# Four chained image layers on one core: scans with their own buffers beside the layers of the next pair of images

## The chip, the cores and the metric

The kernel runs on one core of a Trainium2 chip. The metric is the device time of one execution in microseconds (us); the median of three runs of the kernel before is 18586.44 us (18541.16 to 18590.59). The engines are named as in the profile: PE (matrix products, with PEld for the loading of weights), DVE (vector), ACT (activation functions), POOL (GpSimd) and SP, which here only issues DMAs. Everything is in float32. Work arrays live in SBUF, results of PE land in PSUM (eight banks of 512 float32 for each of 128 partitions), and inputs, outputs and spilled arrays in the memory outside (DRAM).

## The reference

Eight images of 64 channels and 64 x 64 pixels go through four layers, one after the other:

```python
x = _L0_conv_ref(x, ...)   # softmax(x^T x / 8) over all 4096 pixels, weighted sum, 3x3 depthwise conv, 1x1 conv, + x
x = _L1_conv_ref(x, ...)   # two blocks of attention in windows of 8x8 (the second one shifted by 4), each with an MLP
x = _L2_conv_ref(x, ...)   # 9 taps weighted by a filter of the pixel and one of the channel, then a 1x9 convolution, + x
x = _L3_conv_ref(x, ...)   # norm, selective scan in four directions, gating, + x; then pooled depthwise convolutions
```

The scan of layer 3 works on 128 channels per image, four directions k (rows, columns, and both backwards) and 16 states per channel:

```python
h = h * jnp.exp(dt_t[..., None] * A) + dt_t[..., None] * B_t[:, :, None, :] * u_t[..., None]
return (h, jnp.einsum('bkcn,bkn->bkc', h, C_t))
```

over the 4096 pixels in the direction's order. dt is softplus of a projection of u; B and C are projections of u too.

## The kernel before

Two images at a time stand on the 128 partitions (64 channels each). `tile_kernel` (L1551) goes through the four pairs p, and for each runs `layer0_direct`, `layer1_direct`, `layer2` and `layer3` one after the other. Each layer opens its own pools of SBUF and PSUM, which take the place of the layer before; four large buffers ("slabs" of 66 x 66) are shared by all of them.

The kernel is written in a tile language: the source gives instructions with their tiles; a planner sets the order of each engine's queue from the data between instructions, the buffers that are free and its own estimate of durations, with the source's order as priority, and puts in the waits. On the chip each queue runs strictly in that order.

Layer 0 (L585) takes columns of the 4096 x 4096 scores in four blocks of 1024; for each of 32 row tiles PE makes the scores of both images (L637), ACT takes exp with a running sum (L647), and PE adds up the weighted values (L623). `block0` (L568) does the depthwise convolution with nine DVE instructions over the whole image (L433). Layer 1 (L733) goes through eight rows of windows in each of two blocks: `window_head` (L769) makes a norm, queries, keys and values, `window_row` (L819) scores, exp, weighted values and the projection; the head of the next row is called in the middle of the present row (L902). `mlp_direct` (L924) follows. Layer 2 (L1096) takes eight chunks of 512 pixels. Nearly all products of these layers are on PE; POOL has only borders and copies there.

Layer 3 norms (L1187), and then for each of the two images: `mixed` (L1201) makes the 128 channels XC of the scan, `ss2d_direct` (L1271) runs the scan, and `project_out` (L1245) makes the gate, the norm of the result Y and the projection. `safm` (L1488) ends the pair.

A scan has 32 units for an image: four directions of eight chunks of 512 pixels. `group_inputs` (L1302) makes, a unit ahead, dt and dt times u in `du` (L1310 to L1316; the product L1316 reads du and XC, both in SBUF), stores them to DRAM as `rows` (L1322, issued by ACT), and B and C by two further products (L1326, L1328). `group_scan` (L1332) then works in four quarters q. On the 128 partitions stand 16 states x 8 channels, so each channel's dt and dt u must be on 16 partitions: one DMA (L1356, issued by SP) reads 8 rows of 16 KB from `rows` with each row repeated for 16 partitions, 2 MB into `ub`, of which there are two buffers. POOL multiplies by B (L1364, 2048 elements a partition), ACT makes exp(dt A) into PSUM (L1369), DVE scans (L1371, four of 512), ACT keeps the last column as carry (L1373). The product with C is shared: POOL does half from SBUF (L1375), DVE the other half with a copy `pc` of C in PSUM (L1376, made by L1351). PE sums over states into `y` (L1378), and DVE adds y into Y (L1387, L1389), for directions along columns with a stride of 64.

Of the kernel before, what the change touches and what calls it, by code (L numbers as in the profile page):

```python
# [222 lines left out]
class _Net:  # L223
# [104 lines left out]
    def open(self, ctx, direct):  # L328

        pool = ctx.enter_context(self.tc.tile_pool(name="path", bufs=1))  # L330
        if direct:
            with self.tc.tile_pool(name="temp", bufs=1) as temp:
                self.load(temp, (3,))
                self.prepare_windows(pool)
        else:
            self.load(pool, (4,))
            self.prepare_general(pool)
        self.slabs = ctx.enter_context(self.tc.tile_pool(name="slabs", bufs=4 if direct else 5))
# [246 lines left out]
    def layer0_direct(self, p):  # L585

        nc, tc, w = self.nc, self.tc, self.w  # L590
        X = self.flat("X")
        nc.sync.dma_start(X, self.x[2 * p : 2 * p + 2].rearrange("b c h w -> (b c) (h w)"))
        pad = self.slab("att").rearrange("p (h w) -> p h w", w=66)
        self.pad_border(pad, 66)
        VT = self.flat("VT").rearrange("p (t c) -> p t c", c=P)
        NB = 1024
        with ExitStack() as st:
            wk = st.enter_context(tc.tile_pool(name="w0d", bufs=2))
            ps = st.enter_context(tc.tile_pool(name="ps0d", bufs=3, space=PSUM))
            pso = st.enter_context(tc.tile_pool(name="ps0o", bufs=1, space=PSUM))  # L600

            for g in range(4):
                pv = ps.tile([P, 8, P], F32, name="pvd", tag="s")
                for h in range(2):
                    nc.tensor.matmul(
                        pv[:, 4 * h : 4 * h + 4, :], lhsT=self.ones[0:1, :], rhs=self.b1row, start=True, stop=False
                    )
                    for j in range(4 * h, 4 * h + 4):
                        t = 8 * g + j
                        nc.tensor.matmul(  # L610
                            pv[:, j, :], lhsT=X[:, t * P : (t + 1) * P], rhs=self.w1bd, start=False, stop=(j % 4 == 3)
                        )
                nc.scalar.activation(VT[:, 8 * g : 8 * g + 8, :], pv, AF.Relu)

            parts = wk.tile([P, 2, 32, 4], F32, name="parts", tag="parts", bufs=1)
            half = (slice(0, 64), slice(64, 128))
            for jc in range(L // NB):
                po = pso.tile([P, NB], F32, name="pod", tag="po")

                def weigh(t, es):  # L620
                    for h in range(2):
                        for im in range(2):
                            nc.tensor.matmul(  # L623
                                po[half[im], h * CH : (h + 1) * CH],
                                lhsT=VT[:, t, half[im]],
                                rhs=es[im][:, h * CH : (h + 1) * CH],
                                start=(t == 0),
                                stop=(t == 31),
                            )

                last = None
                for t in range(32):
                    ss = [ps.tile([P, NB], F32, name=f"sd{im}", tag="s") for im in range(2)]
                    for h in range(2):
                        o = jc * NB + h * CH
                        for im in range(2):
                            nc.tensor.matmul(  # L637
                                ss[im][:, h * CH : (h + 1) * CH],
                                lhsT=X[half[im], t * P : (t + 1) * P],
                                rhs=X[half[im], o : o + CH],  # L640
                                start=True,
                                stop=True,
                            )
                    es = []
                    for im in range(2):
                        e = wk.tile([P, NB], F32, name="ed", tag="ed", bufs=6)
                        nc.scalar.activation(  # L647
                            e, ss[im], AF.Exp, scale=C**-0.5, accum_out=parts[:, im, t, jc : jc + 1]
                        )
                        es.append(e)  # L650
                    if last is not None:
                        weigh(*last)
                    last = (t, es)
                weigh(*last)
                nr = NB // 64
                nc.vector.tensor_copy(  # L656
                    pad[:, 1 + nr * jc : 1 + nr * (jc + 1), 1:65], po.rearrange("p (h w) -> p h w", w=64)
                )

            sums = self.sums[:, p]  # L660
            nc.vector.tensor_reduce(sums, parts, AX.X, ALU.add)
# [157 lines left out]
    def window_row(self, i, wy, T, now, ahead, wk, ps, pss, psa):  # L819
# [42 lines left out]
        def weigh(x, e):  # L862
# [14 lines left out]
            if x == x4 + 2:  # L877
                normalise(x4, av)
# [710 lines left out]
```

## Time and profile before

| what | value |
|---|---|
| median of 3 runs | 18586.44 us |
| the profiled execution: time, span | 18587.73 us, 18585.9 us |
| mean granted clock of PE | 0.690 |
| busy share of the span: PE, DVE, ACT, POOL | 60%, 47%, 34%, 38% |
| the two DMA queues of SP (q1) and ACT (q10), share of 16 engines' span | 52.8%, 2.2% |
| moved by DMA | 2311.16 MB |
| chain that ended last, by engine | PE 39%, DMA 21%, POOL 18%, DVE 14%, ACT 5%, issue 3% |
| POOL product with B, L1364: number, mean | 1024, 4614 ns |
| POOL product with C, L1375 | 1024, 2342 ns |
| DVE scans, L1371 | 3584 of 1264 ns and 512 of 1204 ns |
| DVE product with C, L1376 | 1024, 1219 ns |
| ACT exp of dt A, L1369 | 4096, 680 ns |

The table of groups in a profile gives for each line and engine how many instructions there were, the time in which at least one ran and the mean of one; PE overlaps its products, so its busy time is less than number times mean. The page cuts the span into 40 slices and gives the busy share of each in tenths; "granted clock" is the share of full speed that PE got. A second view gives the same for stretches that one chooses. The first pair of images takes the stretch from 26 to about 4630 us.

### The profile page before, as it was taken

The page shows a single profiled execution, that of the slowest core. Times are in us where ns is not written, and L with a number is a line of the kernel's source. Part 1 is how long each engine was busy: PE and PEld are TensorE (multiplying, and loading weights), DVE is VectorE, ACT ScalarE, POOL GpSimd, SP SyncE. Part 2 cuts the span into 40 slices and gives each one's busy share as a digit, 9 for nine tenths or more (in the row PEclk, how much of TensorE's full clock was granted, in tenths as well). Part 3 has the DMA queues.
Part 4 walks back from the last instruction along what each step waited for, and adds up shares of the span by engine and source line. Part 5 has one row for each costly group of instructions (what it writes and reads, how often), then busy time and mean ns, then how long its engine had stood idle before and what let it go on. Part 6 is the DMA issues. An engine that isn't in the chain of part 4 may idle for free.

```text
span 18585.9 us, 125685 instructions
## 1 busy us (share of the span) xinstructions
PE 11180.3 (60%) x47382; PEld 3532.5 (19%) x47382; DVE 8741.3 (47%) x8028; ACT 6383.0 (34%) x10722; POOL 7154.4 (38%) x2272
## 2 busy tenths in 40 slices
PE   9895444444989544444498954444459895444444
PEld 3441000001344100000134410000013441000001
DVE  0224665665032466566503246656650324665665
ACT  5432332332543233233255323323325432332332
POOL 0003664664000366466400036646630003664664
PEclk9777666666977666666697766666669766666666
DMA  0005996995000599699500059969950005996995
GB/s 15 1 1 114 213 208 153 214 209 128 1 1 1 115 211 208 153 213 208 129 1 1 1 120 213 209 151 212 209 124 1 1 1 114 213 208 151 212 209 128
DMA packets 221419, 2311.16 MB, mean 124 GB/s; under 512 B 19072, under 2 KB 19200, under 8 KB 88960
## 3 DMA queue, kind: packets, MB, share of 16 engines
q1 hardware_dynamic: 152640, 2164.33, 52.8%
q10 hardware_dynamic: 68160, 138.71, 2.2%
q8 instruction: 373, 6.11, 0.1%
q14 instruction: 246, 2.02, 0.0%
HBM read 2160.35 MB, written 142.61 MB: 124 GB/s over the span
## 4 chain that ended last, share of the span: by engine, by line
PE 39%; DMA 21%; POOL 18%; DVE 14%; ACT 5%; issue 3%; POOLq 0%; SPq 0%; ACTq 0%; DVEq 0%
DMA ub<-rows 21%; POOL vd L1364 13%; DVE hd L1371 9%; PE sd L637 5%; PE pod L623 5%; POOL vd L1375 5%; PE w_av L870 4%; PE pbd L1326 4%; PE yd L1378 3%; PE w_s L834 2%; PE pb L1165 2%; PE acc L1169 2%; PE py L1178 2%; DVE XC L433 2%; DVE cv L433 1%
## 5 line engine op out<-in xcount | busy, mean ns | idle before, releaser
L1378 PE MATMUL yd<-vd,pack 128*32 128x512 f32 x8192 | 3139.7, 1009 | 5708.5 <-POOL vd L1375 5708.1
L1371 DVE TENSOR_TENSOR_SCAN hd<-dad,carry,vd 128x512 f32<-128x512 f32 x3584 | 4306.7, 1264 | 2650.3 <-POOL vd L1364 2650.2
L1364 POOL TENSOR_TENSOR vd<-ub,BC 128x2048 f32<-128x2048 f32 x1024 | 4724.6, 4614 | 1384.4 <-DMA ub<-rows 1374.7
L1369 ACT ACTIVATE dad<-ub,As 128x512 f32<-128x512 f32 x4096 | 2663.9, 680 | 4535.9 <-DVE hd L1371 3676.8
L1375 POOL TENSOR_TENSOR vd<-hd,BC 128x1024 f32<-128x1024 f32 x1024 | 2398.0, 2342 | 3158.8 <-DVE hd L1371 3130.5
L1378 PEld LDWEIGHTS yd<-vd,pack 128*32 128x32 f32 x8192 | 375.1, 137 | 8366.1 <-POOL vd L1375 7291.6
L647 ACT ACTIVATE ed<-sd 128x1024 f32<-128x1024 f32 x1024 | 1039.2, 1020 | 871.3 <-PE sd L637 871.1
L1171 POOL MEMSET act<- 128x32 f32 x32 | 4.0, 125 | 3364.3 <-PE pf2d L938 2480.0
L1376 DVE TENSOR_TENSOR vd<-hd,pcd 128x1024 f32<-128x1024 f32 x1024 | 1248.4, 1219 | 70.3 <-DVE hd L1371 2.8
L637 PE MATMUL sd<-X 64*128 64x512 f32 x4096 | 1041.1, 619 | 7.5 <-ACT ed L647 7.5
L623 PE MATMUL pod<-ed,VT 128*64 128x512 f32 x4096 | 1000.3, 606 | 0.0
L1310 PE MATMUL pdd<-XC,xdt 128*128 128x512 f32 x512 | 470.9, 1013 | 824.7 <-ACT BC L1328 478.7
L417 POOL MEMSET XP<- 128x66 f32 x4 | 0.6, 154 | 2469.2 <-PE n_c L459 2469.2
L1326 PE MATMUL pbd<-XC,pack 128*128 128x512 f32 x1024 | 875.0, 986 | 18.6 <-ACT du L1315 18.6
L1373 ACT ACTIVATE carry<-hd 128x4 f32<-128x4 f32 x896 | 185.1, 207 | 1928.6 <-DVE hd L1371 1928.6
L1371 DVE TENSOR_TENSOR_SCAN hd<-dad,vd 128x512 f32<-128x512 f32 x512 | 584.4, 1204 | 553.0 <-POOL vd L1364 553.0
L870 PEld LDWEIGHTS w_av<-vals,w_e 64*64 64x64 f32 x16384 | 722.8, 174 | 286.3 <-issue 231.0
L656 DVE COPY att<-pod 128x1024 f32<-128x1024 f32 x16 | 19.6, 1226 | 1589.8 <-PE pod L623 1589.7
L870 PE MATMUL w_av<-vals,w_e 64*64 64x9 f32 x16384 | 749.6, 224 | 4.5 <-ACT w_e L859 3.6
L1328 ACT ACTIVATE BC<-pbd 128x512 f32<-128x512 f32 x512 | 305.2, 597 | 885.5 <-POOL vd L1364 646.4
L1389 DVE TENSOR_TENSOR Y<-Y,yd 128x512 f32<-128x512 f32 x192 | 207.2, 1079 | 718.4 <-PE yd L1378 718.3
L637 PEld LDWEIGHTS sd<-X 64*128 64x128 f32 x4096 | 362.2, 187 | 675.9 <-issue 655.1
(244 smaller groups left out, 11356.7 us busy)
## 6 DMA issues: line engine op xcount, KB each, us to landing
ub<-rows SPq DMA_DIRECT2D x1024, 2048.0 KB
rows<-du ACTq DMA_DIRECT2D x512, 256.0 KB
X<-in_x SPq DMA_DIRECT2D x4, 2048.0 KB
out<-Y SPq DMA_DIRECT2D x32, 256.0 KB
pack<-in_w ACTq DMA_DIRECT2D x1, 2691.0 KB
pack<-in_w ACTq DMA_DIRECT2D x1, 1193.0 KB
pack<-in_w ACTq DMA_DIRECT2D x1, 424.5 KB
pack<-in_w ACTq DMA_DIRECT2D x1, 66.0 KB
```

The source lines that it names most:

```text
L433: nc.vector.scalar_tensor_tensor(dst, src, wt[:, t : t + 1], dst, ALU.mult, ALU.add)
L623: nc.tensor.matmul(po[half[im], h * CH : (h + 1) * CH], lhsT=VT[:, t, half[im]], rhs=es[im][:, h * CH : (h + 1) * CH], start=(t == 0), sto ...
L637: nc.tensor.matmul(ss[im][:, h * CH : (h + 1) * CH], lhsT=X[half[im], t * P : (t + 1) * P], rhs=X[half[im], o : o + CH], start=True, stop= ...
L647: nc.scalar.activation(e, ss[im], AF.Exp, scale=C**-0.5, accum_out=parts[:, im, t, jc : jc + 1])
L870: nc.tensor.matmul(av[half[im], x - x4 + j, h, :], lhsT=e[half[im], h // 4, j, h % 4, :], rhs=V[half[im], x + j, h, :], start=True, stop=True,
L1326: nc.tensor.matmul(pb, lhsT=w[name][:, k, :], rhs=xc, start=True, stop=True)
L1364: nc.gpsimd.tensor_tensor(v, ub[:, 1], BB.unsqueeze(1).to_broadcast([P, 4, TD]), ALU.mult)
L1369: nc.scalar.activation(da, ub[:, 0, r], AF.Exp, scale=self.As[:, k, g : g + 1])
L1371: nc.vector.tensor_tensor_scan(along(h[:, r]), along(da), along(v[:, r]), first, ALU.mult, ALU.add)
L1375: nc.gpsimd.tensor_tensor(v[:, 0:2], h[:, 0:2], CC.unsqueeze(1).to_broadcast([P, 2, TD]), ALU.mult)
L1376: nc.vector.tensor_tensor(v[:, 2:4], h[:, 2:4], pc.unsqueeze(1).to_broadcast([P, 2, TD]), ALU.mult)
L1378: nc.tensor.matmul(y[32 * r : 32 * r + 32], lhsT=w["ysel"][:, q, :], rhs=v[:, r], start=(q == 0), stop=(q == 3))
```

## The change

A new class `_Direct` takes the place of the four layers' direct versions; `tile_kernel` calls the front of the next pair (layers 0 to 2 and the inputs of the scan) after the scans of the present one, and the end of layer 3 (`back`) after that.

- **Buffers.** Scans have SBUF and four PSUM banks of their own that stay open for the whole run (Y, carries, pool `scan`, `ps_scan`); the layers have three slabs and four other banks (three of tag f, one accumulator). Layer 0 now takes blocks of 512 columns in place of 1024, the scores of layer 1 two separate banks, the MLP a chunk at a time with norm, Gelu and the reloading of the table (`log_exp`) in each chunk. The next head of layer 1 is called at the end of a row, its queries have one buffer. Convolutions go by 16 rows.
- **Memory between.** The front stores x2 (layer 2's result), and for each image xc (the scan's channels), xt (the same with rows and columns exchanged, turned by an ACT copy) and zs (the gate). A scan loads its 512 columns from xc or xt, contiguous in both cases, and stores ys; `back` loads ys, zs and x2. Each has two buffers in DRAM.
- **Spread.** A quarter is cut in two (rp); each half has two DMAs (s) that read 4 KB rows, 0.5 MB each, into a `ub` of half the size. `rows` are stored by SP in place of ACT.
- **Products.** POOL multiplies 1024 elements at a time, takes three quarters of the product with C, and DVE one quarter; that one reads h and C, both in SBUF. The copy `pc` in PSUM is gone.
- Borders, the copy into XP and the enlarging of the pooled arrays move from POOL to DVE and ACT. The order of directions is 1, 3, 0, 2.

The core of the diff (the removed functions are those printed above; what is left out of layers 0 to 2 computes as before):

```diff
+class _Direct:
...
+        self.dram = ctx.enter_context(tc.tile_pool(name="mem", bufs=2, space=bass.MemoryType.DRAM))
+        one = ctx.enter_context(tc.tile_pool(name="scan1", bufs=1))
+        self.Y = one.tile([P, L], F32, name="Y", tag="Y")
+        self.carries = one.tile([P, 4, 4], F32, name="carry", tag="carry")
+        self.sw = ctx.enter_context(tc.tile_pool(name="scan", bufs=2))
+        self.slabs = ctx.enter_context(tc.tile_pool(name="slabs", bufs=3))
+        self.ps = ctx.enter_context(tc.tile_pool(name="ps_scan", bufs=3, space=PSUM))
+        self.pf = ctx.enter_context(tc.tile_pool(name="ps_front", bufs=3, space=PSUM))
...
+    def mlp(self, i, X, wk):
...
+            for im in range(2):
+                ph = self.bank("ph")
+                nc.tensor.matmul(ph, lhsT=w[f"f1w{i}"][half[im], :], rhs=H[half[im]], start=True, stop=True)
+                h = wk.tile([P, CH], F32, name="hid", tag="hid", bufs=4)
+                g = nc.scalar.activation(h, ph, AF.Gelu, bias=net.bf1[:, i : i + 1])
+                hid.append(h)
+            net.log_exp(g)
...
+    def scan_sources(self, p, X2):
...
+                for s in range(4):
+                    cv = wk.tile([P, 16, 64], F32, name="xcv", tag="xcv")
+                    self.dwconv(cv, pad, 16 * s, 16, w["cw"], w["cb"])
+                    nc.scalar.activation(cv, cv, AF.Silu)
+                    last = nc.scalar.activation(XT[:, 16 * s : 16 * s + 16, :], cv, AF.Copy)
+                    nc.sync.dma_start(xc[:, 1024 * s : 1024 * s + 1024], cv.rearrange("p a b -> p (a b)"))
...
+                    z = wk.tile([P, CH], F32, name="z", tag="z")
+                    last = nc.scalar.activation(z, pz, AF.Silu, bias=w["in_b"][:, 1:2])
+                    nc.sync.dma_start(zs[:, c * CH : (c + 1) * CH], z)
+                net.log_exp(last)
+                self.kept[2 * p + im] = (xc, xt, zs)
...
+    def scans(self, image):
+        xc, xt, _ = self.kept[image]
+        self.out = self.memory("ys")
+        units = []
+        for k in (1, 3, 0, 2):
+            order = range(NTD) if k < 2 else range(NTD - 1, -1, -1)
+            units += [(k, c, at) for at, c in enumerate(order)]
...
+    def inputs(self, image, unit):
...
+        x = wk.tile([P, TD], F32, name="xs", tag="xs")
+        nc.sync.dma_start(x, self.kept[image][k % 2][:, c * TD : (c + 1) * TD])
+
+        pd = ps.tile([P, TD], F32, name="pdd", tag="da")
+        nc.tensor.matmul(pd, lhsT=net.xdt[:, k, :], rhs=x, start=True, stop=True)
+        du = wk.tile([P, 2, TD], F32, name="du", tag="du", bufs=1)
+        nc.scalar.activation(pd, pd, AF.Exp, bias=w["dtb"][:, k : k + 1], accum_out=net.esum[:, image, k, c : c + 1])
+        nc.scalar.activation(du[:, 0], pd, AF.Ln, bias=1.0)
+        nc.vector.tensor_tensor(du[:, 1], du[:, 0], x, ALU.mult)
+
+        rows = self.dram.tile([32, 2, 4, TD], F32, name="rows", tag="rows")
+        for s in range(2):
+            nc.sync.dma_start(rows[:, s].rearrange("m r t -> r m t"), du[:, s])
...
+    def scan(self, nth, unit, ready, ahead):
...
+        for q in range(4):
+            for rp in range(2):
+                ub = wk.tile([P, 2, 2, TD], F32, name="ub", tag="ub")
+                for s in range(2):
+                    nc.sync.dma_start(
+                        ub[:, s].rearrange("p r t -> p (r t)"),
+                        rows[GD * q : GD * q + GD, s, 2 * rp : 2 * rp + 2]
+                        .rearrange("d r t -> d (r t)")
+                        .unsqueeze(0)
+                        .to_broadcast([NST, GD, 2 * TD]),
+                    )
+                v = wk.tile([P, 2, TD], F32, name="vd", tag="v", bufs=3)
+                nc.gpsimd.tensor_tensor(v, ub[:, 1], BB.unsqueeze(1).to_broadcast([P, 2, TD]), ALU.mult)
+                h = wk.tile([P, 2, TD], F32, name="hd", tag="h")
+                for j in range(2):
+                    r = 2 * rp + j
+                    da = ps.tile([P, TD], F32, name="dad", tag="da")
+                    nc.scalar.activation(da, ub[:, 0, j], AF.Exp, scale=net.As[:, k, 4 * r + q : 4 * r + q + 1])
+                    first = 0.0 if at == 0 else self.carries[:, q, r : r + 1]
+                    nc.vector.tensor_tensor_scan(along(h[:, j]), along(da), along(v[:, j]), first, ALU.mult, ALU.add)
...
+                if rp == 0:
+                    nc.gpsimd.tensor_tensor(v, h, CC.unsqueeze(1).to_broadcast([P, 2, TD]), ALU.mult)
+                else:
+                    nc.gpsimd.tensor_tensor(v[:, 0], h[:, 0], CC, ALU.mult)
+                    nc.vector.tensor_tensor(v[:, 1], h[:, 1], CC, ALU.mult)
...
+            if q == 1:
+                following = ahead()
...
+            o = wk.tile([P, TD], F32, name="yo", tag="yo", bufs=1)
+            nc.vector.tensor_tensor(self.img(o), yd, yp, ALU.add)
+            nc.sync.dma_start(self.out[:, c * TD : (c + 1) * TD], o)
...
+    def back(self, p):
...
+                nc.sync.dma_start(X[:, cols], self.kept["x", p][:, cols])
...
+                    nc.sync.dma_start(y, self.kept["y", 2 * p + im][:, cols])
+                    nc.sync.dma_start(z, self.kept[2 * p + im][2][:, cols])
...
 def tile_kernel(ctx: ExitStack, tc: tile.TileContext, x: bass.AP, packs, layout, out: bass.AP):
     net = _Net(ctx, tc, x, packs, layout, out)
     with ExitStack() as path:
         net.open(path, True)
+        d = _Direct(net, path)
+        net.log_exp()
+        d.front(0)
         for p in range(B // 2):
-            t = net.layer0_direct(p)
-            t = net.layer1_direct(t, p)
-            t = net.layer2(t)
-            net.layer3(t, p, True)
+            d.scans(2 * p)
+            d.scans(2 * p + 1)
+            if p + 1 < B // 2:
+                d.front(p + 1)
+            d.back(p)
```

Behind it, in both kernels, stands a second, general path that runs only where a sum of exponentials leaves its range; it doesn't run here.

## The prediction

> **What bounds the kernel now.** I read the 40 slices first, then cut the first pair of images into its stages with the table of busy times by stretch (front: layers 0 to 2 and the scan's inputs; scan of image 0; between; scan of image 1; end of layer 3).
>
> ```profile
> PE   9895444444989544444498954444459895444444
> ...
> DVE  0224665665032466566503246656650324665665
> ...
> POOL 0003664664000366466400036646630003664664
> ...
> DMA  0005996995000599699500059969950005996995
> ```
> ```profile
> 26.00:1601.00 1575.00, 1414.66 (x9037) 615.18 (x9037) 355.56 (x458) 618.24 (x971) 6.57 (x29) 0.82 0.01 2
> 1601.00:2973.00 1372.00, 599.74 (x1272) 103.47 (x1271) 830.27 (x700) 430.59 (x785) 885.18 (x255) 0.62 0.93 208
> 2973.00:3085.00 112.00, 58.51 (x89) 18.41 (x89) 66.82 (x46) 28.39 (x38) 2.86 (x5) 0.61 0.00 0
> 3085.00:4459.00 1374.00, 602.88 (x1280) 104.49 (x1280) 835.84 (x704) 432.88 (x786) 888.02 (x256) 0.63 0.92 208
> 4459.00:4630.00 171.00, 97.19 (x174) 34.11 (x175) 96.23 (x91) 48.53 (x74) 5.56 (x23) 0.72 0.07 25
> ```
>
> After the stretch and its length come busy us of PE, weight loads, DVE, ACT and POOL, then the granted clock, the DMA share and GB/s. The reader is to see two opposite halves. In the front PE is busy 1415 of 1575 us, while POOL and DMA stand still; in a scan the DMA engines are busy 93% of 1372 us, POOL and DVE some 60%, PE 44%. The pattern repeats four times. So today's bound alternates: PE and its chains for some 1,850 us of a pair's 4,604, the spread of dt (ub<-rows) for 2,746.
>
> The DMA rows price that spread:
>
> ```profile
> q1 hardware_dynamic: 152640, 2164.33, 52.8%
> q10 hardware_dynamic: 68160, 138.71, 2.2%
> ```
>
> q1 is SP's queue, nearly all of it ub: 0.528 x 18585.9 / 1024 = 9.58 us for one spread of 2 MB. q10 is ACT's: 0.022 x 18585.9 / 512 = 0.80 us for 256 KB in 2 KB rows. The load of X, also 2 MB in rows of 16 KB but each read once, keeps the queue busy 82.3% of 7 us (4508 to 4515), 5.8 us. So the spread is slow for its bytes, and it is the same row read by sixteen partitions.
>
> **What the change costs per unit.** A unit is one direction and chunk, 32 to an image, 64 to a pair; now 1372/32 = 42.9 us. I work out what each engine must do in a unit if the next pair's front is laid beside it.
>
> DMA now: 4 x 9.58 + 2 x 0.80 = 39.9 (93% of 42.9). Added: the load of xs, 256 KB, 0.80; and through memory x2 twice 2 MB for a pair, and for each image xc, xt, zs, ys written and ys, zs read, 12 MB, in all 28 MB: 112 x 0.80 = 90 us a pair, 1.4 a unit. The spread itself goes from rows of 16 KB to rows of 4 KB, a form the trace doesn't show. Its floor is X's rate, 5.8 us for 2 MB; its ceiling I set at today's 9.58, since the 2 KB rows of q10 (6.4 us for 2 MB) show no loss by short rows. I take 9.58: the same row is still read sixteen times. Sum 42.1; with the floor 27.0.
>
> POOL: 8 products of 1024 at half of L1364's 4.61 (2.31), 4 of 1024 at 2.34 and 4 of 512 at 1.17: 32.5, now 27.7.
>
> DVE: 830.3/32 = 25.9, less four L1376 of 1.22 plus four of 512 at 0.69 (L583's row), and du 1.36 to 0.69 now that x is contiguous: 23.1. The front and end add (355.6 + 66.8 + 96.2)/64 = 8.1: 31.2.
>
> ACT: 430.6/32 = 13.5, some four more carries at 0.21, less the two DMA issues that go to SP; front and end (618.2 + 28.4 + 48.5)/64 = 10.9. Layer 0's exps come in halves: 256 more a pair, with a readout of 0.20 each and two of about 0.60 (L1328's row for 512) for one of 1.02, 97 us a pair; two table loads of 1.28 in each of 16 MLP chunks, 41; the turned copies into XT, two of 4096 at L1217's 3.6, 7. Together 27.
>
> PE: 599.7/32 = 18.7, less pcd 396.8/256 = 1.55, plus (1414.7 + 58.5 + 97.2)/64 = 24.5: 41.7 at today's clocks.
>
> SP: 16 spreads, xs and two rows at 0.51 us to issue, 9.8 us, and some 105 issues of layers and back in a pair, 0.8: no bound. But all of them are now in one queue in order: a store of rows that waits for du, or of xc that waits for a convolution, has the next ub behind it, and POOL's product waits for that. The inputs of a unit are asked for two quarters ahead, some 20 us, which covers the new load of xs; uncovered, 256 x 3 us would be 770.
>
> **A wait that is added.** The second half of h x C moves from pcd, in PSUM, to CC, in SBUF, beside h in SBUF. The one DVE product in today's scan with both operands in SBUF is du:
>
> ```profile
> L1316 DVE TENSOR_TENSOR du<-du,XC x256: 685/1115/5073, 1604.2 to 18284.3; 128x512 f32<-128x512 f32 x128
> ...
> L1376 DVE TENSOR_TENSOR vd<-hd,pcd x1024: 1202/1222/1226, 1637.6 to 18404.9; 128x1024 f32<-128x1024 f32 x171
> ```
> ```profile
> 2005.88 4.53 POOL L1364 TENSOR_TENSOR vd<-ub,BC 128x2048 f32<-128x2048 f32 x1 [0.44 <-DMA ub<-rows]
> 2006.42 4.53 DVE L1316 TENSOR_TENSOR du<-du,XC 128x512 f32<-128x512 f32 x1
> ```
>
> The first fence gives least, median and greatest ns of two lines, the second start and us of two instructions. du takes 0.69 us at its shortest, 5.07 at its longest: begun 0.54 us into a product on POOL it ends 0.54 us after it. L1376, with PSUM, never stretches. So I charge each such operation half a POOL product, 1.17 us, and POOL the operation's own time. In a unit there are five (four CC, one du) and some 200 of the front's in a pair (convolution taps, sums), 3 a unit: DVE 31.2 + 8 x 1.17 = 40.6. POOL stands 5 x 0.69 plus 193/64 (four convolutions of 38 us and 40 us of sums) = 6.5: 39.0.
> The Trainium skill, SBUF — State Buffer, "Who interferes with whom", says the same against this change: a DVE instruction with two SBUF inputs and a GpSimd one that reads SBUF exclude each other for a whole instruction. Without that rule DVE would need 31 a unit and POOL 32.5, and the sum below would not move, since DMA decides it.
>
> PE's 41.7 holds at the clocks of the table above, 0.62 in a scan and 0.82 in the front. Over 60 to 550 us, where PE is busy 488 of 490, the granted clock is 1.00; at that clock in the mixed stage PE would need 17.2 x 0.62 + 24.5 x 0.82 = 31. I keep 31 and 41.7 as ends.
> TensorE: Matmul & The Clock Gate, Part 1, says that idleness throttles the array and activity releases it; by that rule PE, fed from two sides, would need 31 and drop out; the sum would again stay with DMA.
>
> **Does the order allow it?** The queues are in order, so the front can only fill gaps if the planner deals its instructions among the scan's. Today's trace shows that it does so where buffers allow:
>
> ```profile
> 4540.07 2.41 DVE L431 TENSOR_SCALAR S<-F,pack 128x4096 f32<-128x4096 f32 x1 [0.86 <-ACT F L1503]
> 4542.40 2.28 DVE L1514 TENSOR_TENSOR half<-F 128x2048 f32<-128x2048 f32 x1
> 4544.60 4.48 DVE L433 SCALAR_TENSOR_TENSOR S<-F,pack,S 128x4096 f32<-128x4096 f32 x1
> 4549.00 1.22 DVE L1518 TENSOR_TENSOR pool<-half 128x1024 f32<-128x1024 f32 x1
> ```
>
> In the source all nine taps of S stand ahead of half. The change gives scans and layers separate SBUF, four PSUM banks each and memory between, so nothing but data ties them; only z of the next pair (two buffers of zs) waits until back has read the present one.
>
> **Sum.** In the mixed stage DMA 42.1, PE up to 41.7, DVE 40.6 and POOL 39 lie together, so none runs at its bound. Today 39.9 gives 42.9, 8% over. With a spread buffer half as deep (2 x 1 MB) I take 46, a pair's 64 units 2,944 us. The first front stands alone: 1,575 plus 250 for three shared banks in place of eight, heads that follow the row (16 x 10 us) and the MLP's table loads, 1,825. The last pair's scans with back beside them: 64 x 44 = 2,816. Last back 171 + 20. Start 26. Sum 26 + 1,825 + 3 x 2,944 + 2,816 + 191 = 13,690. The profiled execution took 18587.73 (span 18585.9), the median of three is 18586.44; so 26% less.
>
> **Rivals.** (1) The spread in 4 KB rows is fast (X's rate): DMA 27; DVE and PE decide, 40 a unit mixed, POOL's 36 (32.5 + 3.5) plus one at the end: 26 + 1,825 + 7,680 + 2,368 + 191 = 12,090. For it: 9.58 against 5.8 for equal bytes. Against: the repetition stays. 0.25. (2) The front is a chain of short steps; each waits on an engine behind a scan or an exp, and it outlasts the scans: if every step waits as long as it works, 2 x 1,825 = 3,650 a pair, 26 + 1,825 + 10,950 + 2,816 + 191 = 15,810. For it: layer 1 is PE, DVE, ACT by turns with two or three banks. 0.22. (3) Slower, and the change not doing what it says: the planner places a pair's scans ahead of the whole next front on each queue. Then a pair is 1,825 + 2,816 + 191 = 4,832, four 19,350; it decides when less than 250 us of a front is hidden. Against it: the order above. 0.08. The forecast keeps 0.45.
>
> Range 11,700 to 16,000: both unknown spreads and the stretched front, without serial queues. 0.3% is about what a measurement can tell here; chances 0.91, 0.01, 0.08, the middle one from a partial overlap that falls there by chance.
>
> **What would show it.** Right: PE busy in all slices but the last ones and POOL, DMA from slice 5 on; span from the first scan's start to the last's end near 11,600; the new CC product on DVE with a mean above 1.2 and a maximum near 3; ub's queue share times span over 1024 near 9.6 (rival 1: under 7). Rival 2: slices with PE busy and POOL idle between the scans of pairs. Rival 3: today's pattern of slices. Wrong altogether if ACT is the busiest, by table loads between exps and Gelu.

## The result and the profile after

The changed kernel is slower: 19054.22 us median of 4 runs (19042.1 to 19075.24) against 18571.28 (18541.16 to 18590.59) beside it, a ratio of 1.0263 (95% interval 1.0244 to 1.0281). The prediction was 13,690 us, 11,700 to 16,000. The profiled execution has a span of 19073.4 us.

The page of the changed kernel, its slices and SP's queue:

```profile
PE   9878778767677578867678578876768643343334
...
POOL 0000666666630566566640356666560256666662
PEclk9766888866766788877777688886676765555555
DMA  0001666666631666666640566666660366666663
...
q1 hardware_dynamic: 754752, 2483.34, 51.2%
```

The two opposite halves are gone: PE is busy throughout but for the last pair's scans, and POOL and DMA run beside it. So the change does what it says. But where DMA stood at 9 in a scan it now stands at 6, in slices 33 to 39 too, where no front lies beside the scan; q1 moves 15% more bytes than before and is busy for a smaller share. And three notches remain in POOL and DMA (slices 12 and 13, 21 and 22, 31 and 32). The table by stretch has the columns of the one before: the first front; image 0 with layer 0 of the next pair; image 1 with layer 1; what follows it; the last scan; the last end.

```profile
26.00:1905.00 1879.00, 1595.35 (x9114) 639.07 (x9114) 405.95 (x653) 745.56 (x1629) 6.06 (x2) 0.76 0.03 9
1973.00:3705.00 1732.00, 1394.87 (x3209) 279.17 (x3210) 786.48 (x692) 817.76 (x1937) 1074.57 (x495) 0.88 0.65 164
3776.00:5540.00 1764.00, 1231.08 (x6930) 419.93 (x6930) 1054.74 (x1042) 785.47 (x1317) 1072.71 (x495) 0.69 0.64 161
5540.00:6150.00 610.00, 467.56 (x1086) 152.94 (x1086) 206.22 (x265) 181.24 (x241) 16.55 (x6) 0.68 0.10 35
...
17021.00:18772.00 1751.00, 676.35 (x1176) 104.98 (x1176) 805.98 (x688) 448.90 (x862) 1076.52 (x495) 0.56 0.65 163
18772.00:19073.00 301.00, 154.39 (x190) 43.13 (x190) 110.03 (x147) 61.20 (x90) 0.00 (x0) 0.59 0.11 34
```

Three readings. A scan is long with and without company: the mean distance between the ends of two units (DVE's last addition of each) was 42.0 to 42.2 us in all eight scans before, and is 55.8 to 59.7 now, 56.5 in the last scan, which is alone. In that last scan no engine is near full: POOL 1077 of 1751 us, DVE 806, DMA 65%. And 610 us of the second front (the last rows of layer 1, layer 2 and the scan's sources) still stand alone; in the next two pairs the same gap is 758 and 751.

POOL in the last scan, a stretch of a little over two quarters (start, us, then in brackets the idle time before it and what ended it):

```profile
17596.32 2.34 POOL L1661 TENSOR_TENSOR vd<-ub,BC 128x1024 f32<-128x1024 f32 x1
17600.06 1.26 POOL L1677 TENSOR_TENSOR vd<-hd,BC 128x512 f32<-128x512 f32 x1 [1.40 <-DVE hd L1668]
17601.28 2.81 POOL L1661 TENSOR_TENSOR vd<-ub,BC 128x1024 f32<-128x1024 f32 x1
17606.73 2.34 POOL L1675 TENSOR_TENSOR vd<-hd,BC 128x1024 f32<-128x1024 f32 x1 [2.63 <-DVE hd L1668]
17609.02 2.34 POOL L1661 TENSOR_TENSOR vd<-ub,BC 128x1024 f32<-128x1024 f32 x1
...
17619.92 2.34 POOL L1675 TENSOR_TENSOR vd<-hd,BC 128x1024 f32<-128x1024 f32 x1 [3.06 <-DVE hd L1668]
17626.90 2.34 POOL L1661 TENSOR_TENSOR vd<-ub,BC 128x1024 f32<-128x1024 f32 x1 [4.64 <-DMA ub<-rows]
```

L1661 is v, the product with B; L1675 and L1677 are POOL's products with C in the first and second half of a quarter, L1668 the scans. POOL's queue alternates: v of a half, then the product of that half. The product waits for the scans, the scans wait for v, and the next v stands behind the product although its data are there. One after the other a quarter takes v 2.81, two scans 2.63, product 2.34, v 2.34, one scan 1.40, product 1.26: 12.8 us, 51 a unit. That is the **chain theory**. Once a unit there is a stall more, as at 17626.90, for ub.

The rivals: **ring** (with two buffers of 1 MB the spread is asked for too late); **rows** (reads of 4 KB are dear); **lock** (DVE's product from SBUF shuts POOL out); **queue** (stores of rows in SP's queue hold up the spread); and that the **layers** beside the scan hold it up.

### The profile page after: what moved, and what is told of

Same layout as the page of the kernel before. It is cut to its first block, busy times and chain, and to the rows that moved or that the text cites. A ratio compares the mean times of both kernels' runs of the same rounds, so it can differ in the third digit from the quotient of the medians.

```text
span 19073.4 us, 141051 instructions
## 1 busy us (share of the span) xinstructions
PE 12998.2 (68%) x46870; PEld 3672.8 (19%) x46870; DVE 9010.5 (47%) x8876; ACT 7316.1 (38%) x14447; POOL 8967.9 (47%) x4112
## 5 line engine op out<-in xcount | busy, mean ns | idle before, releaser
L1661 POOL TENSOR_TENSOR vd<-ub,BC 128x1024 f32<-128x1024 f32 x2048 | 5276.4, 2577 | 5111.6 <-DMA ub<-rows 5019.0
L1681 PE MATMUL yd<-vd,pack 128*32 128x512 f32 x8192 | 4165.4, 845 | 4558.5 <-POOL vd L1675 2645.0
L1668 DVE TENSOR_TENSOR_SCAN hd<-dad,carry,vd 128x512 f32<-128x512 f32 x3584 | 4407.0, 1269 | 4728.9 <-POOL vd L1661 4570.8
L1675 POOL TENSOR_TENSOR vd<-hd,BC 128x1024 f32<-128x1024 f32 x1024 | 2442.8, 2386 | 3358.5 <-DVE hd L1668 3334.1
L1677 POOL TENSOR_TENSOR vd<-hd,BC 128x512 f32<-128x512 f32 x1024 | 1317.8, 1287 | 1318.5 <-DVE hd L1668 1312.9
L1272 ACT ACTIVATE e<-s 128x512 f32<-128x512 f32 x2048 | 1201.5, 590 | 1564.1 <-PE s L1266 1559.3
L1266 PE MATMUL s<-X 64*128 64x512 f32 x4096 | 1691.8, 695 | 2.3 <-ACT e L1272 2.3
L1258 PE MATMUL po<-e,VT 128*64 128x512 f32 x4096 | 1625.1, 680 | 9.6 <-ACT e L1272 9.5
L1678 DVE TENSOR_TENSOR vd<-hd,BC 128x512 f32<-128x512 f32 x1024 | 1090.5, 1065 | 59.6 <-DVE hd L1668 0.9
L1668 DVE TENSOR_TENSOR_SCAN hd<-dad,vd 128x512 f32<-128x512 f32 x512 | 599.0, 1208 | 737.7 <-POOL vd L1661 687.8
L1627 PE MATMUL pbd<-xs,pack 128*128 128x512 f32 x1024 | 663.2, 738 | 102.5 <-DVE hd L1668 98.8
L1389 PE MATMUL w_s<-w_qx,w_kk 32*64 32x256 f32 x4096 | 548.3, 500 | 33.3 <-DVE w_e L1402 18.1
L1522 PE MATMUL acc<-tap,pack 128*128 128x512 f32 x576 | 496.7, 993 | 0.0
```

Source lines behind the costliest of these rows:

```text
L1258: nc.tensor.matmul(po[half[im]], lhsT=VT[:, t, half[im]], rhs=es[im], start=(t == 0), stop=(t == 31))
L1266: nc.tensor.matmul(ss[im], lhsT=at(half[im], t), rhs=X[half[im], jc * CH : (jc + 1) * CH], start=True, stop=True)
L1272: nc.scalar.activation(e, ss[im], AF.Exp, scale=C**-0.5, accum_out=parts[:, im, t, jc : jc + 1])
L1522: nc.tensor.matmul(acc, lhsT=w["ident"], rhs=tap, start=(t == 0), stop=(t == TAPS - 1))
L1661: nc.gpsimd.tensor_tensor(v, ub[:, 1], BB.unsqueeze(1).to_broadcast([P, 2, TD]), ALU.mult)
L1668: nc.vector.tensor_tensor_scan(along(h[:, j]), along(da), along(v[:, j]), first, ALU.mult, ALU.add)
```

## The experiments

| run | what it is | unit of a lone scan, us | total, us |
|---|---|---|---|
| before / changed | | 42.1 / 56.5 | 18571 / 19054 |
| e1 | before, new scan body | 51.9 | 21030 |
| e2 | e1, four buffers of ub | 51.9 | 20982 |
| e3 | e1, next v ahead of the product | 43.3 | 18808 |
| e4 | e3, four buffers of ub | 36.7 | 17132 |
| e5 | before, spread in 4 KB rows only | 39.0 | 17759 |
| e13 | e1, rows stored by SP | 51.9 | 20999 |
| e6 | changed, rows stored by ACT | 52.3 | 18712 |
| e14 | e6, POOL's order held | 52.6 | 19050 |
| e15 | changed, xs loaded by ACT, order held | 54.4 | 19172 |
| e7 | changed, next v ahead | 47.1 | 17321 |
| e8 | e7, three buffers of ub, rows by ACT | 42.3 | 16644 |
| e9 | changed, front between the scans | 56.5 | 18168 |
| e10 | e8 and e9 | 42.4 | 15928 |
| e11 | e10, next v ahead across units | 42.6 | 15836 |
| e12 | e11, front's stores by ACT | 42.8 | 15819 |

e10, e11 and e12 were timed four times each, the others once, all beside runs of the kernel before on the same chip (18557 to 18582 us). "Unit" is the mean over all eight scans in the kernel before and its variants (e1 to e5, e13), where every scan is alone, and over the last scan in the others.

### The scan body, in the kernel before (e1 to e4)

There, every scan is alone and there is room for buffers. e1 puts the changed body (halves, 4 KB rows, products) into `group_scan`; e2 changes two sizes of it:

```diff
-ub = wk.tile([P, 2, 2, TD], F32, name="ub", tag="ub", bufs=2)
+ub = wk.tile([P, 2, 2, TD], F32, name="ub", tag="ub", bufs=4)
-v = wk.tile([P, 2, TD], F32, name="vd", tag="v", bufs=3)
+v = wk.tile([P, 2, TD], F32, name="vd", tag="v", bufs=4)
```

In e3 the source begins the next half (its spread and its v) ahead of this half's product, and an order, without a wait, is written down between the two POOL instructions (`then`: ic, this half's product, behind the next v):

```diff
+n = 2 * q + rp + 1
+if n < 8:
+    coming.append(begin(n // 2, n % 2))
 if rp == 0:
-    nc.gpsimd.tensor_tensor(v, h, ...)
+    ic = nc.gpsimd.tensor_tensor(v, h, ...)
...
+if n < 8:
+    self.then(ic, coming[-1][2])
```

e4 is e3 with e2's buffers.

> The kernel before with the new scan body alone: quarters in two halves, spread in 4 KB rows into two buffers of 1 MB, POOL three quarters of the product with C, DVE one quarter from SBUF. Layers, their order and their buffers stay as before, nothing runs beside a scan. Chain theory (POOL's queue alternates v of a half and the product of that half, so v, two scans and the product follow one another: 2.35 + 2.46 + 2.34 and 2.35 + 2.46 + 1.26 us a quarter, some 14 with gaps, 56 a unit): 42.1 becomes 56 a unit, 18571 + 256 x 14 = 22150 us. Ring theory (the next spread is issued only when a buffer of 1 MB comes free) and the theories that 4 KB rows or the lock between DVE and POOL cost it: the same 22150. If the loss comes from the layers beside the scan: 18600.

> As e1, but four buffers of ub in place of two and four of v in place of three; the order of POOL's queue is the same (v, product, v, product). Ring theory: a spread is then asked for two halves earlier, the unit falls to the DMA's or POOL's need, at most 45 us, total 19300 or less. Chain theory: unchanged, 56 a unit, within 300 us of e1, since POOL's next v still stands behind the product that waits for the scans. Rows or lock theory: unchanged too.

> As e1 with two buffers of ub, but inside a unit the next half's v is put ahead of this half's product with C in POOL's queue (7 of 8 halves of a unit). Chain theory: DVE finds the next v ready when its two scans are done, the unit falls to 43 to 48 us, total 18800 to 20100. Ring theory: unchanged, since the spread still lands as late as before: within 300 us of e1. Lock theory: unchanged.

> As e3 with four buffers of ub and four of v. Chain theory: as e3 or a little less, 41 to 46 us a unit, 18300 to 19600. Ring theory: as e2. If both are needed (the order shortens the chain and then the ring is late), e2 and e3 each stay above 50 a unit and only this one falls below 45. Lock or rows theory: still near 56 a unit.

The new body alone costs 9.8 us a unit, with no layer beside it; the expected 14 was too much, some 4.5 come from elsewhere. Twice the buffers change nothing (51.9). The order alone gives 8.6 us back, and only then do the buffers count, another 6.6. That is the chain, and behind it the ring. What POOL waited for in the last scan (us in total, times, longest), first e1, then e3:

```profile
POOL vd L1376 <- DVE hd L1370: 337.1, 122, 3.9
POOL vd L1378 <- DVE hd L1370: 171.1, 123, 1.4
```
```profile
POOL vd L1371 <- DMA ub<-rows: 249.2, 184, 5.3
POOL vd L1393 <- DVE hd L1384: 2.8, 8, 0.7
```

In e1 (a window of 1600 us) both products wait for the scans 508 us, and v hardly waits for ub. In e3 (a window of 1200 us) those waits are gone and v waits for the spread: the ring, which e2 couldn't show because the chain hid it. In e4 POOL and the transfer are both near full; its window has POOL busy 952 us of 1000 and DMA 0.97:

```profile
15900.00:16900.00 1000.00, 520.36 (x1028) 77.45 (x1024) 823.99 (x600) 392.86 (x761) 952.16 (x436) 0.59 0.97 244
```

So e4, which has the changed scan body but none of the overlap, is 7.8% below the kernel before in its one run. The lock theory expected no fall in e3 or e4, where DVE's product reads h and C from SBUF as before, so the lock isn't the main cause.

### The spread alone (e5)

One DMA of 2 MB becomes four of 0.5 MB; nothing else changes.

```diff
-ub.rearrange("p s r t -> p (s r t)"), rows[GD * q : GD * q + GD] ...
+for rp in range(2):
+    for s in range(2):
+        ub[:, s, 2 * rp : 2 * rp + 2] ..., rows[GD * q : GD * q + GD, s, 2 * rp : 2 * rp + 2] ...
```

> The kernel before with one part alone: a quarter's spread of 2 MB is read by four DMAs in 4 KB rows instead of one in 16 KB rows; whole quarters, two buffers of 2 MB and the products as before. In the four runs above 2 MB in 4 KB rows kept the DMA engines busy some 8.6 us against 9.58 in 16 KB rows (queue share times span over 1024). If that is the form's own price: the unit falls from 42.1 by up to 4 x 0.95, to 38 to 40 us, total 17550 to 18100. If more issues and more packets cost something: 42 us or more, 18570 and above. No theory of the slowdown needs this run; it prices the spread alone.

42.1 became 39.0. q1 stands in e5 thus:

```profile
q1 hardware_dynamic: 595008, 2164.53, 49.9%
```

0.499 x 17757.3 / 1024 = 8.65 us for 2 MB, against 9.58: the rows theory falls, four DMAs of short rows are 10% faster here than one of long rows.

### Late dt (e13, e6, e14, e15)

What adds 4.5 us between e1 and the last scan of the changed kernel? There POOL waits for ub once a unit, and SP, when it is to store rows, waits about as long in all for DVE and ACT, which make du (62.5 + 44.2 + 36.4 = 143 us):

```profile
POOL vd L1675 <- DVE hd L1668: 360.9, 124, 4.0
POOL vd L1677 <- DVE hd L1668: 170.6, 122, 2.3
POOL vd L1661 <- DMA ub<-rows: 141.3, 32, 6.4
```
```profile
SPq L1623 <- DVE du L1619: 62.5, 29, 2.3
SPq L1623 <- ACT BC L1629: 44.2, 14, 3.2
SPq L1623 <- ACT du L1618: 36.4, 11, 6.3
```

In e6, e13 and e14 the store changes its issuer (e13 the other way), in e15 the load of xs does. In e14 and e15 the order of POOL is held as well, v behind the product before it.

```diff
-nc.sync.dma_start(rows[:, s].rearrange("m r t -> r m t"), du[:, s])
+nc.scalar.dma_start(rows[:, s].rearrange("m r t -> r m t"), du[:, s])
```

And in e15 alone:

```diff
-nc.sync.dma_start(x, self.kept[image][k % 2][:, c * TD : (c + 1) * TD])
+nc.scalar.dma_start(x, self.kept[image][k % 2][:, c * TD : (c + 1) * TD])
```

> The changed kernel, but rows are stored by ACT as before, not by SP. Queue theory: in the last scan POOL waits for ub once in each unit (141 us in 32 units, 4.4 a unit), because the store of rows waits in SP's queue for du with the next spread behind it; that wait was absent from e1, where ACT stores rows. So the unit falls from 56.5 to about 52, total 19054 - 256 x 4.4 = 17930, if the scans set the pace; 18200 if layer 2 alone and the ends stay. If the 4.4 come from something else (the load of xs, the layers beside the scan): unchanged within 200 us.

> As e1, with rows stored by SP in place of ACT; POOL's order is v, product, v, product throughout, as in e1. Queue theory: the store waits for du with the next spread behind it in SP's queue, POOL waits for ub once a unit as in the changed kernel's last scan (4.4 us), and the unit rises from 51.9 to about 56: total 21030 + 256 x 4.4 = 22160. Order theory (the fall from 56.5 to 52.3 in the last scan of e6 came from POOL's order, which changed there too in one half of eight, and the 4.4 us of the changed kernel come from the load of xs or the other stores): the unit stays at 51.9, total within 200 us of 21030.

> As e6 (rows stored by ACT in the changed kernel), but POOL's order is held at v, product, v, product throughout. e13 showed that SP's queue costs nothing where du is early (51.9). In the changed kernel du is late: xs is loaded in SP's queue, its product stands in PE's queue behind the sums of a half. Queue theory, amended (a late du blocks the spread behind its store only in SP's queue): the lone last scan falls from 56.5 to 52 to 53 us a unit. Order theory (e6's fall came from the changed order of POOL): it stays at 56 to 57.

> The changed kernel with the load of xs issued by ACT, rows stored by SP as in the changed kernel, POOL's order held at v, product, v, product. If du is late because xs is loaded in SP's queue behind spreads that wait for buffers: du comes earlier, the store of rows waits no more, the lone last scan falls to 52 to 53 us a unit. If du is late for its place in the queues of PE, ACT and DVE, whenever xs comes: it stays at 56 to 57.

e6's last scan fell to 52.3 as expected, but its total, 18,712, missed both cases, the planner had changed POOL's order too (in one quarter of four the second v came first), and POOL's wait for ub stayed at 139 us. e13 then fell on the other side: SP's store alone costs nothing, and at that store SP waits only this long:

```profile
SPq L1322 <- DVE hd L1370: 2.5, 4, 0.7
```

e14 settles it, with POOL's order held and this wait for ub:

```profile
POOL vd L1670 <- DMA ub<-rows: 14.8, 3, 12.7
```

Both are needed: du must be late, and its store must have the next spread behind it in one queue. How late it is can be read from the trace: in the last scan a unit's du is finished some 100 us before the unit ahead of it ends in e1 and e13, but only some 30 us before that in the changed kernel, e14 and e15. In the stretch shown above du begins on DVE at 17614.61 and takes 2.80 us beside POOL's v; the store is issued behind it, and the spreads from 17618.03. e15 (54.4) takes away about half, between its two cases: SP waits for du some 70 us there in place of 143, but du itself comes no earlier. So that xs in SP's queue makes du late isn't shown; why it is late isn't resolved.

All this holds for the lone scan. Beside the layers e14's units still take 56 to 59 us, and its total didn't move; e6's 342 us went with the changed order. There the wait only changes its place: over the first pair's two scans v's wait for ub falls from 215 us in the changed kernel (1973 to 5540 us) to 12 in e14 (1970 to 5576), and the wait of POOL's two products for the scans rises from 1,133 to 1,380. These runs don't say why.

### The repairs in the changed kernel (e7, e8)

e7 is the order of e3 in `scan`. e8 adds rows by ACT, and

```diff
-ub = wk.tile([P, 2, 2, TD], F32, name="ub", tag="ub")
+ub = wk.tile([P, 2, 2, TD], F32, name="ub", tag="ub", bufs=3)
-with tc.tile_pool(name="w1a", bufs=2) as wk:
+with tc.tile_pool(name="w1a", bufs=1) as wk:
-e = wk.tile([P, 2, 4, 64], F32, name="w_e", tag="w_e", bufs=4)
+e = wk.tile([P, 2, 4, 64], F32, name="w_e", tag="w_e", bufs=2)
-ge = wk.tile([P, 8, 64], F32, name="ge", tag="ge", bufs=2)
+ge = wk.tile([P, 8, 64], F32, name="ge", tag="ge")
```

> The changed kernel with POOL's order as in e3: the next half's v ahead of this half's product, two buffers of ub, rows still stored by SP. Chain theory: 56 falls by the 8.6 us that e3 took off e1, to about 47.5, total 19054 - 256 x 8.5 = 16900; up to 17600 if the layers beside the scan then outlast it. If the layers beside the scan set the pace already: 18800 or more.

> The changed kernel with all three: POOL's order as in e7, three buffers of ub (room from smaller rings in the attention of layer 1 and in the end of layer 3), rows stored by ACT. Chain, queue and ring theory together: the lone last scan at 38 to 43 us a unit, between e3 and e4. Beside the layers the pace is then theirs or PE's, 42 to 50 a unit; total 15000 to 16700. If the layers' chain outlasts the scans, the scans of a pair end well ahead of them and POOL stands idle between pairs for more than the 610 us of the changed kernel: total above 16000 with the last scan still near 40.

e7 came as the chain theory had it: 17,321, the last scan at 47.1 us a unit, the scans beside layers at 50 to 54. e8's 16,644 and its last scan, 42.3, fit both of its cases; but the stretch between pairs grows to 825 and 926 us, which was the sign of the second case, that the layers outlast the scans. Its scans beside layers take 43 to 48: faster scans leave the layers less time to hide in. The smaller rings slow the layers as well, but little: the first front, which stands alone, takes 1,914 us in place of 1,879.

### The layers that stood alone (e9 to e12)

e9 changes the place of a call, and gives the arrays in DRAM four buffers:

```diff
-self.dram = ctx.enter_context(tc.tile_pool(name="mem", bufs=2, space=bass.MemoryType.DRAM))
+self.dram = ctx.enter_context(tc.tile_pool(name="mem", bufs=4, space=bass.MemoryType.DRAM))
 d.scans(2 * p)
-d.scans(2 * p + 1)
 if p + 1 < B // 2:
     d.front(p + 1)
+d.scans(2 * p + 1)
 d.back(p)
```

e10 is e8 with that edit. e11 lets the next v go ahead across the end of a unit, and e12 issues the stores of x2 (now behind H's bias on ACT), xc, xt and zs by ACT:

```diff
 if 2 * q + rp < 7:
     coming = begin(ready, q + rp, 1 - rp)
+elif following is not None:
+    coming = self.coming = begin(following, 0, 0)
...
-nc.sync.dma_start(zs[:, c * CH : (c + 1) * CH], z)
+nc.scalar.dma_start(zs[:, c * CH : (c + 1) * CH], z)
```

> The changed kernel with two edits: in the source the front of the next pair stands between the two scans of a pair, not behind them, and the arrays in DRAM have four buffers in place of two, so that xc, xt and zs of the next pair wait for nobody. Scan body and SP's queue stay as in the changed kernel. Order theory: layer 2 and the scan's sources stand alone after the scans (610, 759 and about 760 us) because the source gives them the last priority, not because no engine has room; with the edit they go into the second scan, no stretch between pairs has POOL idle for more than 200 us, and the unit stays at 56 to 59: total 19054 - 2130 = 16900, up to 17500. Capacity theory (the front cannot go faster beside a scan): the second scan of each pair stretches by as much as is hidden, total 18700 or more.

> The two edits of e9 together with the three of e8 (POOL's order, three buffers of ub, rows stored by ACT). If the causes add: 26 + 1940 of the first front + 4 x 64 units at the 42 to 48 us that e8 showed + 300 of the last end = 13000 to 14600 us. If the front's chain sets the pace once it has no gap of its own (in e8 it took the two scans and 825 to 926 us more, some 3700 us a pair): 26 + 1940 + 3 x 3700 + 2750 + 300 = 16100.

> As e10, with the next v ahead of the product across the end of a unit too (8 halves of 8 in place of 7). Chain theory: one stall of some 4 to 5 us a unit is left in e10 at each unit's end; where the scan sets the pace it goes, 2 to 4 us a unit less: total 500 to 1000 us under e10. If DMA (some 36 us a unit) or the layers set the pace: within 200 us of e10.

> As e11, with the front's stores of x2, xc, xt and zs issued by ACT behind the ACT instruction that makes or uses the data, not by SP. In e11 six units of each second scan, those beside layer 2, take 92 to 116 us, and SP waits 280 us in that scan at the stores of x2, xc and zs with the next spread behind them in its queue. Queue theory: those waits go, three pairs save up to 840 us, total 15000 to 15500. If layer 2 stretches the scan by the work of PE, DVE and ACT itself (their queues hold its steps ahead of the scan's): within 200 us of e11's 15836.

e9 lies between its two theories: the gap, 2,124 us in all, is gone, but only 886 are won, mostly because the second scan of each of the first three pairs now takes 66 us a unit. The source's order left layer 2 alone, but the room for it beside the scan isn't free. (e9 also has more buffers in DRAM. In the changed kernel layer 2, which needs none of them, already stands in the gap.) e10 shows the layers setting the pace, as its second case said: 15,928, with 3,470 to 3,670 us from the first unit of one pair to that of the next. e11 gained 92 us (ratio to before 0.8538, 0.8522 to 0.8554; e10 0.8585, 0.8570 to 0.8599), the second case there too. e12 is within the error of e11 (0.8523, 0.8506 to 0.8539): SP's waits at the front's stores weren't the price. What is can be read from PE in e11, beside layer 2, where a unit takes up to 116 us:

```profile
4853.67 2.84 PE L1527 MATMUL pb<-f,pick 18*128 18x512 f32 x6
4856.44 4.54 PE L1531 MATMUL acc<-tap,pack 128*128 128x512 f32 x6
4860.91 2.84 PE L1527 MATMUL pb<-f,pick 18*128 18x512 f32 x6
...
4871.23 4.40 PE L1531 MATMUL acc<-tap,pack 128*128 128x512 f32 x6
4875.56 1.03 PE L1510 MATMUL p_m<-X,swc 128*18 128x512 f32 x2
4876.43 1.02 PE L1704 MATMUL yd<-vd,pack 128*32 128x512 f32 x2
4877.38 8.06 PE L1540 MATMUL py<-act,pack 128*128 128x512 f32 x18
```

L1704 is the scan's sum over states, and a buffer of v comes free only behind it. In these 32 us PE runs without a gap of more than 0.15 us, 58 products are done (the two lines left out are one more x6 each of L1531 and L1527), and two of them are the scan's. Between 3450 and 5338 us POOL's v waits for yd as follows; another 209 us of its idle time show no releaser.

```profile
POOL vd L1671 <- PE yd L1704: 292.8, 40, 26.4
```

That PE's queue sets the pace there is read from the trace; it was not tested by a run of its own.

e10, e11 and e12 beat both kernels: 14.2%, 14.6% and 14.8% under the one before.

## Why the prediction was wrong, by its steps

**Two steps failed.** The larger one turns the engines' needs into 46 us (mixed) and 44 us (alone) a unit: "Today 39.9 gives 42.9, 8% over". It took the scan to run close to its busiest engine and added something for a smaller buffer. Nothing in it asked in what order POOL's queue would stand once a quarter is cut in two. The measured units are 56 to 60 us (mixed) and 56.5 (alone). The other step is the overlap: the sum has no term for layers that stand alone behind the scans, and 2,124 us of them did. The difference of 5,383 us to the span of the profiled execution is made up like this:

| term | forecast | measured | difference |
|---|---|---|---|
| first front | 1,825 | 1,879 | 54 |
| three pairs' scans beside layers | 3 x 2,944 | 3,635 + 3,706 + 3,711 | 2,220 |
| layer 2 and sources alone | 0 | 615 + 758 + 751 | 2,124 |
| last pair's scans | 2,816 | 3,691 | 875 |
| last end | 191 | 301 | 110 |

- The second and fourth terms are the scan's rate. Of the 14.4 us by which a lone unit grew, 9.8 are the new body (e1), of which POOL's order alone gives 8.6 back (e3): the chain. About 4 are the late du, whose store stands before the next spread in SP's queue (e14). For the mixed units such a split isn't shown: the order alone gives 3 to 7 us back (e7), all three repairs together bring them to 43 to 48 (e8), near the 46 of the forecast. The needs, 31 to 42 us by engine, were no measure of the rate: 56.5 lies above them all. The chain could have been read in the trace of before; a quarter of it, in the last scan:

```profile
17708.10 4.51 POOL L1364 TENSOR_TENSOR vd<-ub,BC 128x2048 f32<-128x2048 f32 x1 [1.27 <-DMA ub<-rows]
17715.24 2.34 POOL L1375 TENSOR_TENSOR vd<-hd,BC 128x1024 f32<-128x1024 f32 x1 [2.64 <-DVE hd L1371]
17717.54 4.52 POOL L1364 TENSOR_TENSOR vd<-ub,BC 128x2048 f32<-128x2048 f32 x1
```

  v 4.5, two scans 2.6, product 2.3 is 9.5 us: as long as the spread's 9.58, and so it hid behind it. In halves, the same loop runs twice a quarter with v at half its length but the wait for scans and the product paid each time: 12.8.
- "SP no bound", 10 us a unit, was right as a load. The prediction named the store of rows that waits for du with the next ub behind it, and then put it at nothing: "The inputs of a unit are asked for two quarters ahead, some 20 us, which covers the new load of xs". That covered the load but not the late du: the queue's order costs 4 us a unit in the lone scan (e14), near the 3 us that it named for the uncovered case.
- "Nothing but data ties them" was half right. Layers 0 and 1 do run beside the scans: of a front of 1,879 us, 1,120 to 1,260 are hidden in each pair, so rival 3 (no overlap) is wrong, though its 19,350 lies near the result by accident. The rest stood behind both scans in the source's priority (e9). Nor is z the only tie through memory: xc and xt have two buffers as well, one for each image of a pair. In the gaps of the changed kernel this tie didn't bind, as layer 2 stands there ahead of the stores of xc and xt.
- Rival 2, the front that outlasts the scans, showed its sign in the changed kernel already: PE busy and POOL idle between pairs. But the source's order had a part in that, and moving the call won back 886 of the 2,124 us (e9). When the scan is repaired the rival is what is left: e10 to e12 lie at 15,819 to 15,928, its price was 15,810. That each step of the front waits as long as it works was not measured.
- The spread: 8.5 to 8.65 us in e1 and e5, near the 9.58 taken, far from the floor of 5.8. Rival 1 is wrong. The sign named for it, q1's share times the span over 1024, is 9.54 in the changed kernel, but q1 carries the other arrays there too.
- The CC product on DVE: 1,065 ns mean and at most 2,847 in the changed kernel, where the sign named was a mean above 1.2 us and a maximum near 3. The median is 693 ns, for the product mostly begins just ahead of POOL's next v, and then it is v that takes longer, 2.8 to 2.9 us in place of 2.34:

```profile
17613.96 0.69 DVE L1678 TENSOR_TENSOR vd<-hd,BC 128x512 f32<-128x512 f32 x1
```
```profile
17613.98 2.88 POOL L1661 TENSOR_TENSOR vd<-ub,BC 128x1024 f32<-128x1024 f32 x1
```

  That is some 0.5 us in each quarter's 12.8. In e4, with POOL busy 95% in the window above, the same operation has these least, median and greatest ns:

```profile
L1396 DVE TENSOR_TENSOR vd<-hd,BC x1024: 691/2622/2881, 1642.3 to 16950.3; 128x512 f32<-128x512 f32 x171
```

  That agrees with SBUF — State Buffer, "Who interferes with whom", of the Trainium skill, cited in the prediction: beside a busy POOL the product takes 2.62 us, about as long as a POOL instruction (2.34), and not 0.69. The charge of 1.17 on top was too small there (the mean is 2.28) and too large in the changed kernel.
- PE's clock did rise when fed from two sides, as the prediction took from the trace of before: 0.88 beside layer 0 and 0.69 beside layer 1 in the first pair, against 0.56 in the lone scan. But PE's time didn't set the pace of the changed kernel: the units beside layers fell by 3 to 7 us with POOL's order alone (e7).
- Of the other signs, PE busy in all but the last slices and POOL and DMA beside it came true, but for the three notches; the span from the first scan's start to the last one's end was to be near 11,600 us and is 16,867 (1905 to 18772).

## What to carry to other kernels

When a loop over engines is cut into finer pieces, write down the in-order queue of each engine for one turn and add up the longest loop through them; the engines' loads say nothing about it, and a loop that is hidden behind a transfer today shows as soon as the transfer gets faster or the pieces smaller. A deeper ring doesn't help while an instruction that could use it stands behind one that waits (e2), and helps a lot once it doesn't (e4). What overlaps is decided by the source's order too: here the call that stood last got only the gaps, and moving it won back less than half of what had stood alone (e9).

## What the runs showed of the hardware that was not expected

- Source rows read by sixteen partitions each were moved faster in short pieces: 2 MB took 9.58 us in one DMA with 16 KB rows and 8.65 in four DMAs with 4 KB rows (e5). Why, and which of the two counts, isn't shown.
- The same store in SP's queue costs nothing or 4 us a unit by how late its data are: SP storing rows left the unit at 51.9 us where du was early (e13), and at 56.5, against 52.6 with ACT storing them (e14), where it was late.
- A product on DVE and one on POOL, both with two inputs in SBUF, lengthen one another by who begins first: the DVE product took 0.69 us and POOL's v 2.88 in place of 2.34 where DVE began 0.02 us ahead, and the DVE product 2.62 (median) beside a POOL that was 95% busy (e4), where it mostly began later than POOL's.
- PE's granted clock was 0.55 in e1's lone scan with PE busy 677 of 1600 us, and 0.94 in e11's first mixed scan with 1132 of 1350.
